# Key loads on another queue, and the heads' projection and some tables at another place, in a four-layer graph network

## The chip, the cores and the metric

The kernel runs on one core of one Trainium2 chip. The metric is the device time of one launch in microseconds (us). The engines are PE (matrix multiplication, with PEld for its weight loads), DVE (the vector engine), ACT (the scalar engine), POOL (GpSimd) and SP (SyncE, which here only issues DMAs). A DMA is issued by the instruction queue of SP, ACT or POOL, and each of these works through its instructions in order: a DMA whose semaphore is not there yet holds everything behind it on that queue.

## The reference

The input is 16 graphs of 1024 nodes with 64 channels, and a weighted adjacency matrix of 1024 x 1024 for each. Four layers follow each other; after each comes `x = layernorm(x + layer(x))`.

```
# layer 0: batch norm, then a residual graph convolution
d = A.sum(2);  A_norm = sqrt(d)[:, :, None] * A * rsqrt(d)[:, None, :]
out = leaky_relu((I - A_norm) @ (batchnorm(x) @ W + b))

# layer 1: attention with 8 heads of 64 channels, gated with the adjacency
attn = softmax(g0 * (q @ k.T) * scale + g1 * A)        # g = exp(x @ W_gamma.T + b)
out  = concat_heads(attn @ v) @ W_proj.T + b_proj

# layer 2: quantiles over the neighbours, then an MLP
nd  = neighbours, thinned where a node has more than 32
s   = sort(where(nd, x, inf)) for each node and channel
agg = sum over tau, w in (.25, .25), (.5, .5), (.75, .25):
          w * (s[floor(pos)] + frac * (s[ceil(pos)] - s[floor(pos)])),  pos = tau * (nv - 1)
out = relu((x + agg) @ W1 + b1) @ W2 + b2

# layer 3
out = A @ (x @ W) + b
```

## The kernel before

A loop `for p in range(B // 2 + 1)`, fully unrolled, works on pairs of graphs, with the stages of three pairs in flight. One iteration holds, in this order:

1. the pool of the sort's keys is opened and `sort_keys` (L1157) loads the key tile (64 channels of two graphs on 128 partitions, 1024 nodes, 512 KB) of pair p-1 from `x2T_d` in HBM, with SP's queue;
2. `layer0` of the two graphs of pair p. `place_tables` (L310 to L317) loads two constant tables, `place` on SP and `identb` on ACT, and DVE makes `negidb` and `noteye` from the second. `layer0` loads x (L407, SP), normalizes it to y on DVE (L410, L411), transposes it on PE (L289), sums the adjacency's rows on ACT (L425, from tiles loaded by ACT's queue, L424), and `neighbours` walks over eight tiles of the transposed adjacency (`at`, L330, SP, four buffers), which give both the thinned neighbour matrix nd (L333, L334, L369) and the convolution's matmuls (L392);
3. `ends(p-2)`: layers 2 (its MLP) and 3 of pair p-2 (loads at L1022, L1023, L1056);
4. `attention(p)` for both graphs, with the sort of pair p-1's 1024 keys of each channel (55 compare-and-swap steps, L1105) beside it on DVE;
5. `quantiles(p-1)`, which finds the wanted neighbours of each node in the sorted order.

**The attention** of a graph runs in steps over head pairs and blocks of 128 queries: scores (L509), exponentials (L516, L524), transposes on PE (L531), and the weighted values (L545), which are a generator `parts` of two halves drained between the next step's transposes. When a graph's eight heads are ready, `heads(gr, k)` for k = 0 to 3 projects them for a quarter of the nodes: 32 matmuls into two PSUM banks (L562), two DVE products with the softmax's reciprocals (`t_pr`, L566), a sum over eight heads (L569), two adds (L570, L571) and the statistics of the layer norm; after k = 3 the norm is applied (L274, L277). For the first graph of a pair, `heads` is called in steps of the second one's attention. For the second graph, the four calls stand at the end of the attention, behind the last weighted values. Then x2 and its transpose are stored by POOL's queue.

**The quantiles** run over 96 steps: 16 groups of four channels, times 3 quantiles, times 2 graphs. In a step, PE makes the products V of nd with the nodes in sorted order, coded in words E (L774 to L779, L838, L847, L848), DVE compares them with limits (`compare`, lt, L853) to find the word in which the wanted rank lies, PE and ACT turn this into a one-hot matrix oh (`one_hot`, L862), DVE picks the words (`pick`, m, L870, twice 128x3072), and PE sums them (`sum_words`, wps). After eight steps of a unit, `kth_bit` finds the bit within the word by a search on DVE (r, L757). Twelve steps after a group's pick comes its lookup: `distances` (from r and the table `pen`), `least_values` and `sum_values` read the values back from tables `bd` and `base` by matmuls (L838) and copies on ACT (L900). Behind the last lookup, DVE scales the result (vals, L919) and POOL stores it (agg_d, L920).

What a unit needs ahead of its steps: `counts` and `limits` (the ranks per node, L659 to L667) and `weights(t)` (L676 to L684, cf among them, which is used from L919 and by the search) for t = 0 to 2; and for each four groups `load_values`, which clears `bd` and `base` with memsets, multiplies `bv` by a constant into `base` on DVE, and has POOL issue eight small DMAs into `bd`. Before the loop over the steps stand the three `weights` and the first three `load_values`.

The order on the engines is set in two ways: a scheduler orders instructions by data and buffers (a tile's slot must be released first), and an order written out by hand, `then`, ties PE's instructions into a sequence. A dependency with `in_order` orders two instructions of one engine and adds no semaphore.

Of the kernel before, what the change touches and what calls it, by code (L numbers as in the profile page):

```python
# [15 lines left out]
BF = mybir.dt.bfloat16  # L16
# [5 lines left out]
ALU = mybir.AluOpType  # L22
AX = mybir.AxisListType
PSUM = bass.MemoryType.PSUM

P = 128
# [12 lines left out]
GB = 4  # L39
# [71 lines left out]
def gnn_kernel(ctx: ExitStack, tc: tile.TileContext, a: dict, out: bass.AP):  # L111
    nc = tc.nc
# [51 lines left out]
    tones4 = load("tones4", [P, 4], F16, a["c_tones4"])  # L164
# [38 lines left out]
    x2T_d = dram.tile([B // 2 * P, N], F32, name="x2T_d")  # L203
# [11 lines left out]
    in_order = mybir.DependencyInfo(mybir.DependencyClass.NoSync, mybir.DependencyReason.DATA)  # L215
# [93 lines left out]
    def place_tables(l0):  # L309
        place = l0.tile([P, 8 * P], BF, name="place")  # L310
        nc.sync.dma_start(place, a["c_place"])
        identb = l0.tile([P, P], BF, name="identb")
        nc.scalar.dma_start(identb, a["c_idb"])
        negidb = l0.tile([P, P], BF, name="negidb")
        nc.vector.tensor_scalar(negidb, identb, -1.0, None, op0=ALU.mult)
        noteye = l0.tile([P, P], BF, name="noteye")
        nc.vector.tensor_scalar(noteye, negidb, 1.0, None, op0=ALU.add)  # L317
        return place, identb, negidb, noteye
# [152 lines left out]
    def attention(nat, ip, graphs, wqkv, x2, beside):  # L471
# [4 lines left out]
        with (tc.tile_pool(name="att", bufs=2, reuse_waits="tile") as att,  # L476
# [75 lines left out]
            def heads(gr, k):  # L552

                if k == 0:
                    nc.vector.reciprocal(gr.sm, gr.sm)
                smv = gr.sm.rearrange("p (f k) (q h) -> p h k f q", f=2, h=2)
                t = att1.tile([P, 2, 2, 4, C], F32, name="t_pr")
                pr = [bank([P, 2, 4, C]) for h in range(2)]
                for f in range(2):
                    for hp in range(H // 2):  # L560
                        for h in range(2):
                            then(nc.tensor.matmul(pr[h][:, f, hp, :],  # L562
                                                  gr.o[hp][HALF[h], (4 * f + k) * P:(4 * f + k + 1) * P],
                                                  wp[HALF[h], hp, :], start=True, stop=True))
                for h in range(2):
                    nc.vector.tensor_tensor(t[:, :, h], pr[h],  # L566
                                            smv[:, h, k, :, :, None].to_broadcast([P, 2, 4, C]), ALU.mult)
                x = gr.xg[:, k]
                nc.vector.tensor_reduce(x, t.rearrange("p f h q c -> p f c (h q)"), AX.X, ALU.add)  # L569
                nc.vector.tensor_tensor(x, x, bp_r[:, None, :].to_broadcast([P, 2, C]), ALU.add)  # L570
                nc.vector.tensor_tensor(x, x, gr.x1[:, k], ALU.add)  # L571
                if k == 0:
                    gr.norm = norm_tiles()
                norm_stats(gr.norm, gr.xg, [k])
                if k == 3:
                    norm_apply(gr.norm, by_half(x2)[:, :, :, gr.bb, :], gr.xg)

            g0, g1 = graphs
# [15 lines left out]
            parts = iter(())  # L594
            for st, (gr, hp, nh, k4) in enumerate(steps):
# [26 lines left out]
                if gr is g0 and hp == H // 2 - 1:  # L622

                    k = 4 * nh + k4
# [4 lines left out]
                if (nh, k4) in ((0, 2), (1, 0)):  # L629
                    if hp + 1 < H // 2:  # L630
                        project(gr, hp + 1, nh)
                    elif gr is g0:
                        project(g1, 0, nh)
            for _ in parts:
                pass
            for k in range(4):
                heads(g1, k)
            nc.gpsimd.dma_start(x2_d[ds(ip * P, P)], x2)
            x2T = att1.tile([P, N], F32, name="t_pr")
# [142 lines left out]
    def quantiles(ip, rk, u_w, b_w):  # L782
# [12 lines left out]
        with ExitStack() as es:  # L795
# [10 lines left out]
            def load_matrix(gr):  # L806
# [4 lines left out]
                for c4 in range(4):  # L811
                    for pc in range(3):
                        nc.gpsimd.dma_start(gr.bv[c4::4, :, pc:pc + 1],
                                            scratchb[gr.r, pc, :].rearrange("(g k) (t u) -> k t g u", k=4, u=1)[c4])

            def load_values(gr, gb):


                bd = gr.bd[gb] = qn.tile([P, 2, GB, P], F16, name="bd", bufs=3)
                nc.vector.memset(bd, 0.0)  # L820
                gs = slice(GB * gb, GB * (gb + 1))
                for c4 in range(4):
                    p4 = slice(c4 * 32, (c4 + 1) * 32)
                    for pc in range(2):
                        nc.gpsimd.dma_start(
                            bd[c4::4, pc, :, p4],
                            scratch[gr.r, pc, :].rearrange("(g k) (t u) -> k t g u", k=4, u=R)[c4][:, gs])
                base = gr.base[gb] = qn.tile([P, GB, 3, 60], F16, name="base", bufs=3)
                nc.vector.memset(base, 0.0)
                nc.vector.tensor_tensor(base[:, :, :, 28:32], gr.bv[:, gs, :, None].to_broadcast([P, GB, 3, 4]),  # L830
                                        tones4[:, None, None, :].to_broadcast([P, GB, 3, 4]), ALU.mult)

# [32 lines left out]
            def pick(u, s):  # L865
                gr, g, q = u.pairs[s]
                u.m = [None, None]
                for kk in range(2):
                    u.m[kk] = qe.tile([P, NW, N], BF, name="m", bufs=2)
                    nc.vector.tensor_tensor(u.m[kk], gr.V[g].bitcast(BF),  # L870
                                            u.oh[s][:, kk, None, :].to_broadcast([P, NW, N]), ALU.mult)

            def sum_words(u, s):
# [38 lines left out]
            def sum_values(u, s):  # L912
# [4 lines left out]
                if s == U8N - 1:  # L917
                    res = qn.tile([P, 512], F32, name="vals", bufs=5)
                    nc.vector.tensor_tensor(res, u.acc, gr.cf[u.n % 3], ALU.mult)  # L919
                    nc.gpsimd.dma_start(agg_d[gr.bb][:, u.n, :], res)  # L920

            pairs = [(gr, g, q) for gr in graphs for g in range(G) for q in range(NQ)]
            groups = [(gr, g) for gr in graphs for g in range(G)]
            units = [SimpleNamespace(n=i // U8N % NU, pairs=pairs[i:i + U8N], oh=[], vals={}) for i in range(0, len(pairs), U8N)]
# [34 lines left out]
                counts(hf)  # L959
            for q in range(NQ):  # L960
                limits(q)
            for t in range(3):
                weights(t)
            more_words(4)
            compare(*steps[0])
            one_hot(*steps[0])
            pen = qn.tile([P, U8N, 3, P], F16, name="pen")
            nc.sync.dma_start(pen, a["c_pen"])
            lookups = [(gr, gb) for gr in graphs for gb in range(G // GB)]
            for _ in range(3):  # L970
                load_values(*lookups.pop(0))
            search = None
            for i, (u, s) in enumerate(steps):
                if i == 3 * NQ:
# [7 lines left out]
                gb, at = divmod(i - U8N - 2 * NQ, GB * NQ)  # L982
                if at == 0 and gb >= 1 and lookups:
                    load_values(*lookups.pop(0))
                look = steps[i - U8N - PARTS] if i >= U8N + PARTS else None
                more = MORE[s]
                pick(u, s)
# [166 lines left out]

    def sort_keys(srt, ip):
        key = srt.tile([P, N], F32, name="key", bufs=2)
        nc.sync.dma_start(key, x2T_d[ds(ip * P, P)])  # L1157
        return key

    def middle(keys, srt, key, pace=()):  # L1160
# [99 lines left out]
```

## Time and profile before

| | us |
|---|---|
| three runs | 13429.87, 13438.83, 13460.58 |
| median | 13438.83 |
| profiled execution | 13430.77 |
| its span in the profile | 13428.9 |

| engine | busy, us | share |
|---|---|---|
| PE | 12106.3 | 90% |
| DVE | 10731.4 | 80% |
| ACT | 7230.1 | 54% |
| POOL | 635.6 | 5% |

An iteration takes about 1645 us: the first quantile words E follow the attention at 1204.7, 2846 and 4491 us. PE's granted clock is 0.948 of full speed in the mean. A line such as "PE bank L838 <- DVE r L757: 18.2, 1, 18.2" in the waits says that PE at line 838 was idle for 18.2 us in total, once, until DVE finished r at line 757. In the timeline each line is start, length, engine, source line, operation, what it writes and reads, and in brackets the idle time before it.

### The profile page before, as it was taken

The numbers are of one execution on the slowest core, as the hardware profiler recorded it, in microseconds if no ns is written. First come the engines' busy times: TensorE is split into PE (matmuls) and PEld (weight loads), VectorE is DVE, ScalarE is ACT, GpSimd is POOL, SyncE is SP. The second block draws the span as 40 slices with busy tenths as digits, with TensorE's granted clock in tenths as the row PEclk, the third lists the DMA queues.
The fourth block names the chain that finished last, engine by engine and source line by source line (L and its number), as shares of the span: only waits on it lengthen the run. The fifth ranks groups of instructions, "written<-read, shape, count | busy, mean of one in ns | idle before, by whom it ended". The sixth has DMA issues, their size and how long they took to land.

```text
span 13428.9 us, 216352 instructions
## 1 busy us (share of the span) xinstructions
PE 12106.3 (90%) x85632; PEld 5237.5 (39%) x85632; DVE 10731.4 (80%) x18699; ACT 7230.1 (54%) x13164; POOL 635.6 (5%) x948
## 2 busy tenths in 40 slices
PE   7898997989979899798997989979899799993998
PEld 4554332543325433253333633335333353331332
DVE  3587887778877788777886788877888778978895
ACT  5665554655536555365553655546455465551553
POOL 0000000000000000000000010000100001000000
PEclk9999998999989999899998999989999899996998
DMA  2110003100031000310004100041000310002001
GB/s 78 69 63 19 5 5 105 57 17 5 5 121 42 15 6 5 131 34 14 5 5 132 32 14 5 5 134 38 6 5 20 121 36 7 8 22 77 4 5 44
DMA packets 356375, 510.90 MB, mean 38 GB/s; under 512 B 124448, under 2 KB 279584, under 8 KB 353312
## 3 DMA queue, kind: packets, MB, share of 16 engines
q1 hardware_dynamic: 288656, 371.94, 8.6%
q10 hardware_dynamic: 34192, 87.14, 1.9%
q0 software_dynamic: 32512, 38.00, 1.1%
q8 instruction: 673, 11.03, 0.3%
q14 instruction: 342, 2.80, 0.1%
HBM read 380.32 MB, written 116.59 MB: 37 GB/s over the span
## 4 chain that ended last, share of the span: by engine, by line
PE 66%; DVE 14%; issue 8%; DMA 3%; ACT 3%; POOL 0%; SPq 0%; DVEq 0%; ACTq 0%; POOLq 0%
PE bank L838 31%; PE acc L838 8%; PE banks L509 6%; PE bank L545 6%; PE bank L531 6%; PE wps L838 3%; DVE m L870 2%; DMA at<-in_adjT 2%; DVE key L1105 2%; PE bank L392 1%; PE bank L488 1%; PE banks L369 1%; PE bank L847 1%; DVE lt L853 1%; DVE mask L1105 1%
## 5 line engine op out<-in xcount | busy, mean ns | idle before, releaser
L870 DVE TENSOR_TENSOR m<-V,oh 128x3072 bf16<-128x3072 bf16 x1536 | 2640.2, 1753 | 312.9 <-PE wps L838 289.3
L838 PE MATMUL bank<-ndT,E 128*128 128x512 fp8e4 x11904 | 2751.7, 381 | 7.3
L900 ACT ACTIVATE vals<-bank 128x512 f32<-128x512 f32 x3072 | 1591.8, 602 | 1399.0 <-PE bank L838 1397.0
L516 DVE CUSTOM_DVE_ANT_0 s<-banks,adj 128x1024 f32<-128x1024 f32 x1024 | 1214.5, 1222 | 801.4 <-PE banks L509 798.4
L848 ACT ACTIVATE V<-bank 128x512 uint16<-128x512 f32 x1536 | 911.8, 597 | 1742.1 <-PE bank L838 1642.4
L838 PEld LDWEIGHTS <-E 128*128 128x128 bf16 x11904 | 1117.9, 98 | 1788.6 <-issue 551.0
L862 ACT CAST oh<-bank 128x512 f16<-128x512 f32 x3072 | 1577.6, 601 | 297.5 <-PE bank L838 297.3
L838 PE MATMUL bank<-oh,bd 128*128 128x512 f16 x6144 | 1480.0, 384 | 0.0
L535 ACT COPY pT<-bank 128x512 f32<-128x512 f32 x1536 | 800.6, 594 | 800.0 <-PE bank L531 799.9
L524 ACT ACTIVATE s<-s,mx 128x1024 f32<-128x1024 f32 x1024 | 1176.8, 1161 | 90.1 <-DVE mx L516 89.2
L509 PE MATMUL banks<-kT,qT 64*128 64x512 f32 x4096 | 1094.5, 625 | 65.7 <-DVE mx L516 36.1
L853 DVE TENSOR_TENSOR lt<-V,lim 128x2048 bf16<-128x2048 uint16 x768 | 935.1, 1218 | 221.5 <-PE bank L838 220.3
L531 PEld LDWEIGHTS bank<-ident,s 128*128 128x128 f32 x8192 | 883.9, 141 | 409.9 <-issue 285.7
L531 PE MATMUL bank<-ident,s 128*128 128x128 f32 x8192 | 1017.0, 277 | 9.3 <-ACT s L524 8.7
L545 PE MATMUL bank<-pT,v 128*64 128x256 f32 x8192 | 991.7, 385 | 0.0
L838 PEld LDWEIGHTS <-bd 128*128 128x128 f16 x6144 | 542.6, 98 | 889.4 <-issue 354.2
L838 PE MATMUL bank<-lt,dif 128*128 128x512 bf16 x3072 | 813.2, 381 | 51.9 <-DVE lt L853 30.9
L838 PE MATMUL acc<-vals,bonesf 128*32 128x512 f32 x6144 | 847.6, 603 | 0.0
L838 PE MATMUL wps<-m,tonesb 128*32 128x512 bf16 x9216 | 641.6, 382 | 78.7 <-DVE m L870 78.7
L838 PE MATMUL bank<-r,pen 32*128 32x512 f16 x6144 | 487.7, 384 | 241.0 <-DVE r L757 226.9
L545 PEld LDWEIGHTS bank<-pT,v 128*64 128x64 f32 x8192 | 544.7, 136 | 306.9 <-ACT pT L535 41.3
L838 PE MATMUL acc<-oh,base 128*32 128x512 f16 x9216 | 641.8, 384 | 0.0
(248 smaller groups left out, 13323.0 us busy)
## 6 DMA issues: line engine op xcount, KB each, us to landing
at<-in_adjT SPq DMA_DIRECT2D x256, 512.0 KB, 5.5
masks_d<-mask SPq DMA_DIRECT2D x440, 128.0 KB, 1.7
mask<-masks_d SPq DMA_DIRECT2D x440, 128.0 KB, 2.1
adj<-in_adj SPq DMA_DIRECT2D x96, 512.0 KB, 5.3
ad<-in_adj ACTq DMA_DIRECT2D x64, 512.0 KB, 6.4
agg_d<-vals POOLq DMA_DIRECT2D x96, 256.0 KB, 2.3
agg<-agg_d ACTq DMA_DIRECT2D x16, 1536.0 KB, 8.0
nd_d<-nd SPq DMA_DIRECT2D x128, 128.0 KB, 1.9
```

Of the source, the lines that this page charges most:

```text
L509: then(nc.tensor.matmul(ss[h][:, hf * 512:(hf + 1) * 512], gr.qk[hp, 0][HALF[h], k * P:(k + 1) * P], gr.qk[hp, 1][HALF[h], hf * 512:(hf + ...
L516: last = nc.vector.tensor_tensor_reduce(s, ss[h], gr.adj[k], -1.0, 3.0e38, ALU.add, ALU.min, mx)
L524: then_act(nc.scalar.activation(s, s, AF.Exp, bias=mx, scale=-1.0, accum_out=sm))
L531: then(nc.tensor.transpose(ps[:, m, :], exps[h][0][:, (4 * mh + m) * P:(4 * mh + m + 1) * P], ident))
L535: then_act(nc.scalar.copy(dst, ps))
L545: then(nc.tensor.matmul(po[HALF[h]], gr.v[:, 4 * mh + m, (2 * hp + h) * C:(2 * hp + h + 1) * C], pT[h][mh][:, m, :], start=(mh == 0 and m ...
L838: then(nc.tensor.matmul(*args, **kw))
L848: nc.scalar.activation(gr.V[g][:, w, cols], ps, AF.Copy, bias=OFF)
L853: nc.vector.tensor_tensor(u.lt, gr.V[g][:, None, 0, :].to_broadcast([P, 2, N]), gr.lim[q], ALU.is_lt)
L862: nc.scalar.copy(oh[:, kk, cols], ps)
L870: nc.vector.tensor_tensor(u.m[kk], gr.V[g].bitcast(BF), u.oh[s][:, kk, None, :].to_broadcast([P, NW, N]), ALU.mult)
L900: nc.scalar.activation(vals[t], ys[t], AF.Relu)
```

## The change

Five edits:

- `identb` is loaded by SP's queue and not by ACT's.
- In `heads`, the sum over eight heads (a reduction of 128x1024 to 128x128) is written as three adds of 128x512, 128x256 and 128x128.
- At the end of the attention, the first half of the last weighted values is followed by `heads(g1, 0)` and `heads(g1, 1)`, then comes the second half, then `heads(g1, 2)` and `heads(g1, 3)`.
- In `quantiles`, the first three `load_values` stand in steps 2, 4 and 6, and `weights(1)` and `weights(2)` in steps 10 and 12; the DVE instructions of `load_values` are ordered behind the latest pick.
- `sort_keys` loads the key by POOL's queue and not by SP's.

```diff
-        nc.scalar.dma_start(identb, a["c_idb"])
+        nc.sync.dma_start(identb, a["c_idb"])
...
                 x = gr.xg[:, k]
-                nc.vector.tensor_reduce(x, t.rearrange("p f h q c -> p f c (h q)"), AX.X, ALU.add)
+                nc.vector.tensor_tensor(t[:, :, 0], t[:, :, 0], t[:, :, 1], ALU.add)
+                nc.vector.tensor_tensor(t[:, :, 0, 0:2], t[:, :, 0, 0:2], t[:, :, 0, 2:4], ALU.add)
+                nc.vector.tensor_tensor(x, t[:, :, 0, 0], t[:, :, 0, 1], ALU.add)
...
+
+            next(parts)
+            for k in range(2):
+                heads(g1, k)
             for _ in parts:
                 pass
-            for k in range(4):
+            for k in range(2, 4):
                 heads(g1, k)
...
+            def behind(i):
+                tc.add_manual_dep(i.ins, picked.ins.name, in_order, reason="after a pair's words")
+
             def load_values(gr, gb):
                 bd = gr.bd[gb] = qn.tile([P, 2, GB, P], F16, name="bd", bufs=3)
-                nc.vector.memset(bd, 0.0)
+                behind(nc.vector.memset(bd, 0.0))
...
-                nc.vector.memset(base, 0.0)
-                nc.vector.tensor_tensor(base[:, :, :, 28:32], gr.bv[:, gs, :, None].to_broadcast([P, GB, 3, 4]),
-                                        tones4[:, None, None, :].to_broadcast([P, GB, 3, 4]), ALU.mult)
+                behind(nc.vector.memset(base, 0.0))
+                behind(nc.vector.tensor_tensor(base[:, :, :, 28:32], gr.bv[:, gs, :, None].to_broadcast([P, GB, 3, 4]),
+                                               tones4[:, None, None, :].to_broadcast([P, GB, 3, 4]), ALU.mult))
...
-            for t in range(3):
-                weights(t)
+            weights(0)
...
-            for _ in range(3):
-                load_values(*lookups.pop(0))
...
+                if i in (2, 4, 6):
+                    load_values(*lookups.pop(0))
+                if i in (10, 12):
+                    weights(i // 2 - 4)
...
         key = srt.tile([P, N], F32, name="key", bufs=2)
-        nc.sync.dma_start(key, x2T_d[ds(ip * P, P)])
+        nc.gpsimd.dma_start(key, x2T_d[ds(ip * P, P)])
```

More of the change, by code (lines that the diff above doesn't have):

```diff
@@ L867, in pick @@
                 u.m = [None, None]
+                nonlocal picked
                 for kk in range(2):
                     u.m[kk] = qe.tile([P, NW, N], BF, name="m", bufs=2)
-                    nc.vector.tensor_tensor(u.m[kk], gr.V[g].bitcast(BF),
+                    picked = nc.vector.tensor_tensor(u.m[kk], gr.V[g].bitcast(BF),
                                             u.oh[s][:, kk, None, :].to_broadcast([P, NW, N]), ALU.mult)
@@ L920, in sum_values @@
                     nc.gpsimd.dma_start(agg_d[gr.bb][:, u.n, :], res)
+            picked = None
             pairs = [(gr, g, q) for gr in graphs for g in range(G) for q in range(NQ)]
```

## The prediction

> **What bounds the kernel now.** I read the page's busy times and its chain first, then the chain, the waits and the timeline at the three places that the diff touches. 0.2% of the time is 27 us, about what a measurement of this kernel can tell from no change.
>
> ```profile
> PE 12106.3 (90%) x85632; PEld 5237.5 (39%) x85632; DVE 10731.4 (80%) x18699; ACT 7230.1 (54%) x13164; POOL 635.6 (5%) x948
> PE 66%; DVE 14%; issue 8%; DMA 3%; ACT 3%; POOL 0%; SPq 0%; DVEq 0%; ACTq 0%; POOLq 0%
> ```
>
> PE carries two thirds of the chain, and the change takes no matmul away. So it can win only where PE waits: at seams between stages, once per pair of graphs. None of these is large against a pair's 1645 us.
>
> Seam 1, the end of attention, from the chain of waits at 1160 to 1240 us (start, length, work):
>
> ```profile
> 1178.88 5.33 PE bank L545 x48
> 1184.22 1.98 PE bank L562 x32
> 1186.20 1.28 DVE t_pr L566 x2
> 1187.50 1.93 DVE xg L569
> ...
> 1191.50 1.79 DVE xg L569
> ...
> 1195.37 1.76 DVE xg L569
> ...
> 1199.20 1.75 DVE xg L569
> ...
> 1204.70 0.60 DVE E L774
> ```
>
> From 1186.2 to 1204.7 the vector engine works alone through four `heads` (L562 to L571) and the norm, and PE waits for it (the stretch holds 18.0 us of DVE in 18.7). The four reductions are 7.23 us of it.
>
> Seam 2, the start of the quantiles, 1231 to 1340 us, PE's waits (total, times, longest), then DVE's for 1224.4 to 1336.3:
>
> ```profile
> PE bank L838 <- DVE r L757: 18.2, 1, 18.2
> PE wps L838 <- DVE m L870: 4.7, 5, 2.3
> PE bank L838 <- DVE lt L853: 3.6, 4, 2.1
> ```
>
> ```profile
> DVE E L777 <- PE bank L838: 2.5, 2, 1.5
> DVE m L870 <- PE wps L838: 2.3, 2, 1.1
> DVE lt L853 <- PE bank L838: 1.5, 1, 1.5
> DVE E L779 <- PE bank L838: 0.5, 2, 0.3
> ```
>
> PE's long wait ends with the first search (r, L757, at 1336.4). Before it DVE idles 6.8 us in 112: DVE's own work sets when that search ends, not PE's.
>
> Seam 3, from the quantiles to the next pair's layer 0, the timeline at 2185 to 2232 us:
>
> ```profile
> 2196.45 0.33 SPq L1157 DMA_DIRECT2D key<-x2T_d  x1
> ...
> 2197.31 0.97 SPq L407 DMA_DIRECT2D x<-in_x  x2
> ...
> 2198.33 3.42 SPq L330 DMA_DIRECT2D at<-in_adjT  x4
> ...
> 2199.41 0.54 POOL L920 DMA_DIRECT2D agg_d<-vals  x1 [38.52 <-DVE vals L919]
> ...
> 2207.52 0.69 DVE L410 TENSOR_TENSOR y<-x,bn_a 128x512 f32<-128x512 f32 x1 [4.31 <-DMA x<-in_x]
> ```
>
> The key's load holds SP's queue for 32.1 us (SP's waits name PE, L838: the last lookup still reads `bd` in the key's space). The table, x and the first adjT tiles stand behind it, though their own buffers are free. They all start at 2196 to 2202, the DMA engines are then 96% busy at 326 GB/s until 2236 (windows), the last adjT tile of the graph is used at 2230.2, and PE waits 11.1 us for y.
>
> [...] the trace's 128x512 add takes 0.69. [...] in this trace x2T_d's stores on POOL land in 3.7 us and the key's loads on SP in 3.6[...]
>
> **The change part by part.** All sums are against the profiled execution: 13430.8 us (span 13428.9); the median of the other runs, 13438.8, is 8 us above it.
>
> *Adds for the reduction.* 128x512 costs 0.69 (key row, L1105), 128x256 0.42 (L428), 128x128 0.29 (L570): 1.40 against 1.81 in the tail, so 4 x 0.41 = 1.6 us per tail. The other 32 of 64 reductions lie beside PE-bound attention steps: nothing. *Order of heads.* Of the 48 L545 matmuls in 5.33 us, 16 now come after the first two heads, so the vector chain starts 5.33/3 = 1.8 us earlier. But PE then runs k=1's matmuls (which wait for a bank that t_pr frees), the 16, a copy on ACT (0.6) and k=2's 1.98 us, ready 7.1 us after the start, where DVE has done its two heads in 6.4: a new stall of 0.7. Tail: 1.6 + 1.8 - 0.7 = 2.7, with a step-by-step run of the chain 2.9; 1.5 if the order stalls more, 3.6 if not at all. Seven tails (pairs 1 to 7; pair 0's is counted below): **20 us** (10 to 25).
>
> *Later tables and weights.* Two of three `weights` (1.85 us each on DVE) and three `load_values` (1.04 each: two memsets and a product) move. Before, the load_values ran while DVE waited for PE and ACT at 1206 to 1228, for nothing; now 3.1 us of them stand inside DVE's full stretch, at steps 2, 4 and 6. The weights were in the stretch and stay in it (steps 10, 12). For that, the first compare no longer stands behind them: the picks and PE's steps begin some 4 us earlier (PE's 7.4 us a step, waits on lt and m less). What counts is the search: DVE's work after 1224.4 grows by 3.1, its 6.8 us of idle shrinks to perhaps 2.5. Gain 6.8 - 2.5 - 3.1 = 1.2 us; all idle gone +3.5, little of it gone -1.5. The lookups' DMAs (8 x 0.54 us of POOL per load) are wanted at step 12, 40 us after the last issue, and POOL has nothing else until then. Eight starts: **10 us** (-12 to 28).
>
> *Keys on POOL, the small table on SP, pairs 2 to 7.* SP is free from 2164: place, identb, x and four adjT tiles (2.5 MB) leave about 32 us earlier, in a third-busy DMA stretch (0.33 of 2150 to 2196). The key leaves on POOL behind the last agg_d store, about 2200.0 instead of 2196.45, and lands at 2203.7 to 2207. In the changed program's order DVE still has mask, key, y, key, y (L1105, L410, L411), so PE's first matmul follows the mask by 3.1 us: 2206.8 to 2210.1 against 2209.5, a gain of 0 to 2.7 where 4.3 of x's wait went. Behind that, 2.5 MB at 330 GB/s are 7.5 us less in the full stretch, but the `ad` tiles on ACT's queue, issued behind hnT, set the second y (2221.9), and four steps of 1.98 us follow: the adjT tail comes 2 to 4 us earlier, not 7.5. DVE is 96% busy at 2236 to 2306, so the shift carries on. I take 3 (-1 to 6); six times: **18 us** (-6 to 36). The identb edit alone is nothing: it leaves with the table, long before DVE reads it.
>
> *Pair 1.* There the key waits for its own data (x2T_d, 71.9 us of SP's wait) until 623.4, and DVE waits 12.6 for it; the key cannot come earlier, but adjacency and table can. They compete with x2T_d: **3 us** (0 to 7) beyond its tail. *The last pair.* No layer 0 follows; the key leaves behind the store, 3 us later, part of it covered by a 4.3 us wait on the masks: **-1** (-3 to 0).
>
> Sum 20 + 10 + 18 + 3 - 1 = 50: 13430.8 - 50 = **13381 us**. All ends good: 96, 13335; all bad: -10, 13441.
>
> **Rivals.**
> (A) *Everything lands.* Quantile starts keep the 4 us of PE's cadence because the search hides behind steps that PE still owes, and the DMA relief brings 6 each: 25 + 28 + 36 + 7 = 96 us, 13335. For it: PE is 90% busy; against: the 18.2 us wait on r.
> (B) *The seams swallow it.* DVE's idle refills behind PE (new waits on m), and the late key eats the earlier x: only tails count, 13411, or less where heads stall: within 0.2%. For it: three waits end together at 2207 to 2210.
> (C) *Slower: the late key.* POOL's path enters the full DMA stretch behind a 256 KB store (8.7 us until used, by the chain) and a 1.5 MB agg load; DVE's in-order mask holds y, and so all of layer 0. It decides where the mask starts after 2206.4 (2209.5 - 3.1). At a landing of 2213, 6.6 us late x 7 = 46, with 3.1 x 8 = 25 of load_values uncovered against 20 of tails: 13431 + 46 + 25 - 20 = 13482; with the threshold just passed, 13440 to 13460. Against it: SP's key landed in 3.6 to 4.0 among the same loads.
> (D) *The change does not do what it says:* tiles' slots still hold x and adjT until 2196. The program's waits for these name work long done, so I give it little; it would cost seam 3's 18: 13399.
>
> **How the numbers follow.** Forecast and D, gains of 28 to 75: 0.57; A: 0.13; B: 0.18; C: 0.12. Faster by over 0.2% takes the forecast and A: 0.70; same: 0.18; slower: 0.12. The range runs from A's end, 13335, to 13435, B and the near part of C.
>
> **What would show it.** In the profile after: DVE adds of 0.69, 0.42 and 0.29 us at the tail and E (L774 before) about 2.9 us sooner after the last transposes; L838's wait on r a little shorter (15 to 18 us) and the first wps 4 us earlier; SP's x and adjT issued near 2165, key on POOL near 2200, y not waiting for x, DMA share under 0.9 at 2196 to 2236. I am wrong if the key's mask starts over 10 us after the last vals, if DVE's time from lim to r grows, or if k=2's matmuls wait over 2 us.

## The result, and the profile after

| | before | changed |
|---|---|---|
| median of 12 runs, us | 13448.07 | 13444.57 |
| lowest and highest, us | 13429.87, 13460.58 | 13422.64, 13458.61 |
| ratio changed : before, 95% interval | | 0.9997 (0.9990 to 1.0005) |
| profiled execution, us | 13430.77 | 13445.01 |

The change makes no difference that can be measured: 4 us faster, with an interval from 13 faster to 7 slower. I had forecast 13381, 50 us faster, in a range of 13335 to 13435; the gain did not come and the time lies outside the range. The profiled execution of the kernel before is one of its fastest, 17 us below the median of 12, so the two profiles are compared place by place and never by their spans. Ratios below are turned into us with 13446.

The page after, busy time of each engine (before: PE 12106.3, DVE 10731.4):

```profile
PE 12131.7 (90%) x85551; PEld 5255.1 (39%) x85632; DVE 10695.0 (80%) x18827; ACT 7227.6 (54%) x13164; POOL 637.3 (5%) x956
```

DVE has 36 us less to do, the same tasks otherwise, and the kernel is no faster. The three seams tell why. Line numbers of the kernel after are higher: L774 is L780, L838 is L847, L870 is L880, L1105 is L1117 and L1157 is L1169 there.

**Seam 1, the end of attention.** PE's timeline of the kernel after at 1186 to 1200 us, and four pairs of graphs later, at 7770 to 7790 us (start, length, line, operation, count):

```profile
1192.76 2.00 PE L562 MATMUL bank<-wp,o 64*128 64x64 f32 x30 [0.56 <-DVE t_pr L566]
1194.68 1.95 PE L545 MATMUL bank<-pT,v 128*64 128x256 f32 x16
...
7775.93 3.10 PE L562 MATMUL bank<-wp,o 64*128 64x64 f32 x30 [0.56 <-DVE t_pr L566]
7778.96 3.68 PE L545 MATMUL bank<-pT,v 128*64 128x256 f32 x16
```

The 16 matmuls of weighted values that were put between the heads take 1.95 us in the first place and 3.68 in the second, and the heads' 30 ahead of them 2.00 and 3.10. First the windows of both places (length, then busy time and count of PE, PEld, DVE, ACT and POOL, PE's granted clock, DMA share and GB/s), then what DVE waits for PE at 1190 to 1208 and at 7772 to 7796 us:

```profile
1192.76:1196.63 3.87, 3.87 (x48) 2.98 (x48) 3.73 (x10) 0.00 (x0) 0.00 (x0) 1.00 0.00 0
7776.60:7782.60 6.00, 6.00 (x40) 3.99 (x38) 5.06 (x15) 0.00 (x0) 0.00 (x0) 0.50 0.01 3
```

```profile
DVE t_pr L566 <- PE bank L562: 4.8, 1, 4.8
```

```profile
DVE t_pr L566 <- PE bank L562: 8.0, 3, 4.8
```

In the second place the clock is halved, and DVE waits 3.2 us more for PE. From the end of the last exponential to the first E, all seven tails of the kernel before last 26.97 us. After, four last 23.68 and three 26.91: 3.3 us won or nothing.

**Seam 2, the start of the quantiles**, from the first limit (lim) to the end of the first search (r). First the window of the kernel before, then that of the kernel after:

```profile
1224.40:1336.20 111.80, 82.10 (x449) 32.13 (x447) 104.09 (x141) 52.15 (x93) 11.25 (x19) 0.92 0.02 2
```

```profile
1229.80:1342.60 112.80, 82.36 (x449) 32.17 (x447) 106.97 (x150) 52.14 (x93) 12.94 (x24) 0.91 0.02 2
```

DVE's work grew by 2.9 us (nine instructions: the three load_values), its idle time fell from 7.7 to 5.8 only, and the stretch is longer, 112.6 in the mean of seven against 111.8.

**Seam 3, from the quantiles to layer 0.** Timeline of the kernel after at 2203 to 2219 us:

```profile
2204.85 0.34 ACTq L1038 DMA_DIRECT2D agg<-agg_d  x1
2204.91 0.69 DVE L929 TENSOR_TENSOR vals<-acc,cf 128x512 f32<-128x512 f32 x1 [38.43 <-PE acc L847]
...
2206.49 0.55 POOL L1169 DMA_DIRECT2D key<-x2T_d  x1
...
2214.53 0.69 DVE L1117 TENSOR_TENSOR mask<-key 128x512 f16<-128x512 f32 x1 [8.59 <-DMA key<-x2T_d]
2215.74 0.68 DVE L410 TENSOR_TENSOR y<-x,bn_a 128x512 f32<-128x512 f32 x1
...
2217.68 1.11 PE L289 MATMUL bank<-ident,y 128*128 128x128 f32 x4 [12.80 <-DVE y L411]
```

x is there long before, and nobody waits for it any more. But y stands behind the sort's first mask on DVE, and the mask waits for the key, which lands 8.0 us after its issue (3.6 before). The windows from the key's issue to its landing, before and after:

```profile
2196.50:2200.10 3.60, 1.89 (x20) 0.52 (x12) 0.69 (x1) 3.54 (x7) 0.54 (x1) 1.00 0.72 237
```

```profile
2206.50:2214.50 8.00, 0.00 (x0) 0.00 (x0) 0.00 (x0) 0.67 (x2) 0.54 (x1) 0.68 1.01 332
```

After, the DMA engines are full all that time and move 2.7 MB, of which the key is 0.5. PE's wait for y is 12.8 us, longer than the 11.1 it had. L289 starts 12.3 us behind the last vals in the mean of pairs 2 to 7, against 10.0.

**Pair 1**, timeline after at 612 to 643 us:

```profile
614.58 3.02 SPq L424 DMA_DIRECT2D adj<-in_adj  x6
619.77 0.54 POOL L651 DMA_DIRECT2D x2T_d<-t_pr  x1 [0.70 <-ACT t_pr L650]
...
632.56 0.54 POOL L1169 DMA_DIRECT2D key<-x2T_d  x1 [12.25 <-DMA x2T_d<-t_pr]
636.70 0.69 DVE L1117 TENSOR_TENSOR mask<-key 128x512 f16<-128x512 f32 x1 [18.65 <-DMA key<-x2T_d]
```

SP no longer waits, so 3 MB of adjacency leave ahead of the 512 KB store of x2T_d that the key itself needs. The store lands after 12.5 us (7.4 before), and DVE waits 18.7 us for the key (12.6 before).

### The profile page after: what moved, and what is told of

The parts are those of the page before. It is cut to its first block, busy times and chain, and to the rows that moved or that the text cites. A ratio compares the mean times of both kernels' runs of the same rounds, so it can differ in the third digit from the quotient of the medians.

```text
span 13443.2 us, 216369 instructions
## 1 busy us (share of the span) xinstructions
PE 12131.7 (90%) x85551; PEld 5255.1 (39%) x85632; DVE 10695.0 (80%) x18827; ACT 7227.6 (54%) x13164; POOL 637.3 (5%) x956
## 5 line engine op out<-in xcount | busy, mean ns | idle before, releaser
L880 DVE TENSOR_TENSOR m<-V,oh 128x3072 bf16<-128x3072 bf16 x1536 | 2639.4, 1752 | 290.9 <-PE wps L847 266.1
L847 PE MATMUL bank<-ndT,E 128*128 128x512 fp8e4 x11904 | 2751.4, 381 | 7.6
L847 PEld LDWEIGHTS <-E 128*128 128x128 bf16 x11904 | 1118.1, 98 | 1798.2 <-issue 561.1
L847 PE MATMUL bank<-oh,bd 128*128 128x512 f16 x6144 | 1482.7, 385 | 0.0
L509 PE MATMUL banks<-kT,qT 64*128 64x512 f32 x4096 | 1088.8, 623 | 68.2 <-DVE mx L516 38.0
L531 PEld LDWEIGHTS bank<-ident,s 128*128 128x128 f32 x8192 | 886.0, 141 | 400.7 <-issue 290.1
L531 PE MATMUL bank<-ident,s 128*128 128x128 f32 x8192 | 1017.6, 278 | 0.5 <-DVE pT L537 0.5
L847 PEld LDWEIGHTS <-bd 128*128 128x128 f16 x6144 | 543.1, 99 | 893.3 <-issue 360.4
L847 PE MATMUL bank<-lt,dif 128*128 128x512 bf16 x3072 | 819.9, 384 | 60.9 <-DVE lt L862 48.2
L847 PE MATMUL acc<-vals,bonesf 128*32 128x512 f32 x6144 | 849.4, 603 | 0.0
L847 PE MATMUL bank<-r,pen 32*128 32x512 f16 x6144 | 489.5, 386 | 243.3 <-DVE r L763 229.3
L847 PE MATMUL wps<-m,tonesb 128*32 128x512 bf16 x9216 | 644.4, 384 | 66.8 <-DVE m L880 66.7
L847 PE MATMUL acc<-oh,base 128*32 128x512 f16 x9216 | 642.1, 384 | 0.0
```

What stands on the lines that cost most here:

```text
L509: then(nc.tensor.matmul(ss[h][:, hf * 512:(hf + 1) * 512], gr.qk[hp, 0][HALF[h], k * P:(k + 1) * P], gr.qk[hp, 1][HALF[h], hf * 512:(hf + ...
L531: then(nc.tensor.transpose(ps[:, m, :], exps[h][0][:, (4 * mh + m) * P:(4 * mh + m + 1) * P], ident))
L847: then(nc.tensor.matmul(*args, **kw))
L880: picked = nc.vector.tensor_tensor(u.m[kk], gr.V[g].bitcast(BF), u.oh[s][:, kk, None, :].to_broadcast([P, NW, N]), ALU.mult)
```

## The experiments

All are timed against the kernel before on the same chip (its medians there are 13443 to 13447 us); the notation is ratio, interval, us. Four of the runs (e10, e11, e12, e18) have 5 executions each, the others 9 to 21. The ratios are not those of the medians: by medians the last row is -54 and e14_adds -30.

| run | edits against the kernel before | ratio (95%) | us |
|---|---|---|---|
| e1_heads | adds, order of heads | 0.9977 (0.9970 to 0.9983) | -31 |
| e14_adds | adds | 0.9975 (0.9967 to 0.9983) | -34 |
| e16_order | order of heads | 0.9997 (0.9989 to 1.0006) | -4 |
| e2_tables | weights and load_values late | 1.0009 (1.0003 to 1.0016) | +12 |
| e6_weights | weights late | 0.9981 (0.9974 to 0.9987) | -26 |
| e17_load_values | load_values late | 1.0027 (1.0017 to 1.0037) | +36 |
| e3_queues | key on POOL, identb on SP | 1.0018 (1.0011 to 1.0025) | +24 |
| e8_identb | identb on SP | 1.0019 (1.0012 to 1.0026) | +26 |
| e11_keys_pool | key on POOL | 1.0033 (1.0021 to 1.0046) | +44 |
| e5_key_act | key on ACT, pairs 2 to 8 | 1.0007 (0.9998 to 1.0015) | +9 |
| e4_keys_on_sp | the changed kernel, key on SP | 1.0007 (0.9999 to 1.0015) | +9 |
| e13_identb_both | identb on SP, a spare one on ACT | 1.0013 (1.0007 to 1.0020) | +17 |
| e15_identb_pinned | identb on SP, ad held behind hnT | 0.9993 (0.9984 to 1.0001) | -9 |
| e10_best | adds, order, weights, key on ACT | 0.9963 (0.9951 to 0.9976) | -50 |
| e12_heads_weights | adds, order, weights | 0.9952 (0.9939 to 0.9964) | -65 |
| e18_adds_weights | adds, weights | 0.9954 (0.9941 to 0.9966) | -62 |

The changed kernel is heads + tables + queues: -31 + 12 + 24 = +5, measured -4 (-13 to +7). So the question "where did 50 us go" has a plain answer: one group gained, two lost. What follows is why.

### The three groups apart

**e1_heads**: the diff's two edits in `heads` and at the attention's end, nothing else.

> The kernel before with the heads' edits alone (three adds, and heads in two parts). Theory 1 (the seams add up, and the changed kernel loses what the heads gain at the other seams): from the last transposes to E is 3.3 us shorter in each of seven tails, as in the changed kernel's trace, and pair 0's tail brings some 3 more: 23 to 27 us faster, ratio 0.998. Theory 2 (an earlier end of the attention is absorbed by later waits or by the clock of TensorE, whatever the other edits do): the same 3.3 us at each tail, but within 8 us of the kernel before in time.

31 us faster; theory 1 on the time. Its tails, though, were not all 3.3 us shorter: 23.7, 25.3 or 26.9.

**e2_tables**: the diff's edits in `quantiles` alone.

> The kernel before with the quantiles' edit alone (tables and weights of later lookups made in the first steps). Theory 1: from lim to the first r it is longer by 0.3 to 1.1 us, since DVE's work there grows by 3 us and its idle time shrinks by 2 only: 3 to 10 us slower over eight starts. Theory 2 (the prediction's): the idle time shrinks by 4 us, 10 us faster. Theory 3: it is free here, and the longer stretch in the changed kernel came from the other edits: no change within 3 us.

12 us slower, theory 1. lim to r lasts 112.5 us (111.8) in the mean of seven starts: DVE works 107.0 us of it and is idle 5.5 (104.1 and 7.7 before). At the eighth start it is 112.8 against 110.2, so the eight together are 7 us longer, inside the interval of 4 to 22.

**e3_queues**: the two changed DMA lines alone.

> The kernel before with the two queue edits alone (keys on POOL, identb on SP). Theory 1: for pair 1 the freed loads crowd out the store of x2T_d and the key's mask is 10 us later; for pairs 2 to 7 the key lands 8 us after its issue instead of 4, L289 is 2 us later each; for the last pair 5 us: 20 to 27 us slower, ratio 1.0015 to 1.002. Theory 2 (the prediction's): x's earlier load and the lighter DMA stretch win, 20 us faster. Theory 3: it is slower at these places, but the layer-0 stretch behind them gives it back: within 8 us.

24 us slower, theory 1. L289 is 12.1 us behind the last vals (10.0), the key lands in 7.8 to 8.3 us for pairs 2 to 8, and the delay does not vanish behind it: the attention starts 221.9 us after the last vals instead of 217.9 (means of six; single ones of the kernel before lie between 214.8 and 220.2).

**e4_keys_on_sp**: the changed kernel with one line back.

```diff
-        nc.gpsimd.dma_start(key, x2T_d[ds(ip * P, P)])
+        nc.sync.dma_start(key, x2T_d[ds(ip * P, P)])
```

> The changed kernel with the keys' load back on SP's queue and the rest as changed. Theory 1 (the key's queue eats the heads' gain): 20 to 25 us faster than the changed kernel, 15 to 22 faster than the kernel before; layer 0's first L289 stands against the last vals as in the kernel before (10.4 us), and 17 us after the norm for pair 1. Theory 2 (the losses come from elsewhere, the tables' edit or chance): like the changed kernel, within 8 us of the kernel before.

9 us slower than the kernel before, with an interval from 1 faster to 20 slower: theory 1 is out, and theory 2 did not name the cause. The key lost nothing here (its mask starts 1.1 us after vals), but L289 was still 11.8 us behind them. Of the queue edits only identb was left to cost time; with e8_identb below the sum is -31 + 12 + 26 = +7.

### Heads: the adds, not the order

**e14_adds**: heads in one part.

```diff
-                nc.vector.tensor_reduce(x, t.rearrange("p f h q c -> p f c (h q)"), AX.X, ALU.add)
+                nc.vector.tensor_tensor(t[:, :, 0], t[:, :, 0], t[:, :, 1], ALU.add)
+                nc.vector.tensor_tensor(t[:, :, 0, 0:2], t[:, :, 0, 0:2], t[:, :, 0, 2:4], ALU.add)
+                nc.vector.tensor_tensor(x, t[:, :, 0, 0], t[:, :, 0, 1], ALU.add)
```

> The three adds alone, with the heads in one part behind the last weighted values. Theory 1 (the sum of the prediction): 1.6 us of the 3.3 at each of eight tails, 13 us faster, the rest of the heads' 31 comes with the order. Theory 2 (the order of heads is what counts, since the chain on DVE starts earlier, and PE hides the rest): under 5 us faster. Theory 3 (the adds free DVE also inside the attention's steps): over 20 us faster.

34 us faster, all that both edits bring: theory 3, and the term of theory 1 with it. All seven tails are 25.31 us, 1.66 shorter, as the prediction's 4 x 0.41 said; that is 13 us over eight. The rest is inside the attention, where I had put nothing. PE's waits at 790 to 1178 us (total, times, longest), first of the kernel before:

```profile
PE banks L509 <- DVE mx L516: 5.0, 6, 1.1
PE bank L531 <- ACT s L524: 1.1, 1, 1.1
PE bank L488 <- DVE t_pr L566: 1.0, 1, 1.0
PE bank L488 <- DVE pT L537: 0.5, 1, 0.5
```

and of e14_adds:

```profile
PE banks L509 <- DVE mx L516: 7.0, 7, 2.9
PE bank L488 <- DVE pT L537: 0.5, 1, 0.5
PE bank L488 <- DVE t_pr L566: 0.3, 1, 0.3
```

The wait of the transposes (L531) for an exponential is gone, and that of L488 for the bank that t_pr frees fell to a third. (L509's 2.9 us wait is in the kernel before too, at 789 us, just outside the window; over pairs 2 to 7, L509's wait for mx is 3.4 us before and 3.7 with the adds.) From the first scores to the last exponential, PE's idle time in the attentions of pairs 2 to 7 is 5.8 us each before and 4.3 with the adds; it is 5.7 to 5.8 in all ten other kernels without the adds and 4.3 to 4.4 in all six others with them. So the reductions of the first graph's heads were not all beside the work: some held DVE in front of something that PE wanted next. 1.66 + 1.5 us over eight pairs are 25 us, inside the interval of 23 to 44.

**e16_order**: the reduction kept.

```diff
+            next(parts)
+            for k in range(2):
+                heads(g1, k)
             for _ in parts:
                 pass
-            for k in range(4):
+            for k in range(2, 4):
                 heads(g1, k)
```

> The heads in two parts alone, with the reduction. Theory 1 (the prediction's): the vector chain starts 1.8 us earlier and stalls 0.7: 1.1 us at each of eight tails, 9 us faster. Theory 2 ([...]3.68 us instead of 1.95 for 16 matmuls; the vector chain waits for them): tails fall on two lengths, one 1.6 us below and one up to 1.6 above the 26.97 of the kernel before: within 6 us of the kernel before.

4 us faster, within its interval of no change: theory 2 on the time, though its shorter length is not there. Six of seven tails are 27.6 us, longer than before, and the seventh is 26.1. With the adds as well (e1_heads, the changed kernel) the tails are 23.68, 25.32 or 26.91. The clock records tell the three apart: at 23.68 the clock is full up to the last of the 16 matmuls; at 25.32 it halves 0.1 to 0.2 us after their start, for 3.41 us; at 26.91 it halves 2.0 to 3.0 us ahead of them, while the second head call's matmuls run, for 6.83 us. At all of these early falls PE was idle for only 0.56 of the 3.41 us before (3.41 us is the shortest stretch of half clock seen), in its wait for t_pr, and worked nearly all the rest on the heads' matmuls (L562).

In the clock records, the stretches of half clock around the tails of these runs last 3.41, 6.83, 10.24, 13.65 or 17.07 us, one to five times 3.41, and the same instructions take 1.95 us in one place and 3.68 in another. Which length a tail gets differs from pair to pair and from run to run: in e10_best all seven are short. What makes the clock fall was not shown.

### Tables: the weights gain, the load_values lose more

**e6_weights**:

```diff
-            for t in range(3):
-                weights(t)
+            weights(0)
...
+                if i in (10, 12):
+                    weights(i // 2 - 4)
```

> The kernel before with weights(1) and weights(2) in steps 10 and 12, and the load_values left where they were. Theory 1 (the moved load_values, which had lain in DVE's idle time, are what made the tables' edit slow): lim to r is 2 us shorter than in the kernel before, about 110 us instead of 111.8, 10 to 20 us faster over eight starts. Theory 2 (DVE's idle time before the first search is set by PE's cadence, whatever stands in it; the weights only move within it): lim to r within 0.5 us of 111.8, no change within 6 us.

26 us faster: theory 1, and more than the 10 to 20 that it gave. The window of this run from lim to r:

```profile
1230.50:1339.00 108.50, 81.75 (x449) 32.20 (x447) 103.96 (x141) 52.11 (x93) 10.90 (x18) 0.92 0.02 2
```

DVE's work is what it was (104.0); its idle time fell from 7.7 to 4.5, and 3.2 us over eight starts are 26. The first pick hardly moves (7.9 us after the first limit, 8.8 before), but the second starts at 16.4 us instead of 19.4: the two late weights are worked off between the picks, and DVE's waits for PE at L777 and L870 fall from 4.8 to 2.0 us in this window.

**e17_load_values**: with the three weights before the loop, and the load_values behind the latest pick as in the change.

```diff
-            for _ in range(3):
-                load_values(*lookups.pop(0))
...
+                if i in (2, 4, 6):
+                    load_values(*lookups.pop(0))
```

> The first three load_values in steps 2, 4 and 6 behind the latest pick, and the weights left before the loop. Theory 1 (their 3.1 us stand in DVE's full stretch and displace nothing): lim to r 115 to 116 us instead of 111.8, 25 to 35 us slower over eight starts. Theory 2 (they fill idle time there when the weights are early, and only with late weights they cost): lim to r within 1 us of 111.8, within 8 us.

36 us slower, theory 1. Its window:

```profile
1235.30:1351.30 116.00, 82.56 (x449) 32.04 (x447) 107.09 (x150) 52.12 (x93) 12.98 (x24) 0.91 0.02 2
```

3.0 us more of DVE's work and 1.2 more of idle time: 4.2 at this start, 4.0 in the mean of seven, and 5.9 at the eighth: 34 us. The two edits add up: 36 - 26 = +10, together +12. Whether the place in the steps or the order behind the latest pick costs the 1 us of idle time was not tried apart.

### Queues: the small table and the key

**e8_identb**: the key still on SP.

```diff
-        nc.scalar.dma_start(identb, a["c_idb"])
+        nc.sync.dma_start(identb, a["c_idb"])
```

> The kernel before with identb on SP's queue alone, behind the blocked key. Theory 1 (one more DMA ahead of x on the blocked queue, and x lands later in the full DMA stretch): L289 is 1.6 us later behind the last vals at six transitions, as in the run with the keys on SP: about 10 us slower. Theory 2 (that 1.6 us came with the tables' edit): no change within 4 us.

26 us slower, for a load of 32 KB, more than either theory gave it: L289 is 12.4 us behind the last vals (10.0). Timeline at 2201 to 2217 us:

```profile
2202.21 0.42 SPq L313 DMA_DIRECT2D identb<-in_c_idb  x1
2202.68 0.97 SPq L407 DMA_DIRECT2D x<-in_x  x2
...
2203.33 0.69 DVE L919 TENSOR_TENSOR vals<-acc,cf 128x512 f32<-128x512 f32 x1 [38.38 <-PE acc L838]
...
2206.40 0.33 ACTq L424 DMA_DIRECT2D ad<-in_adj  x1
...
2214.04 0.69 DVE L410 TENSOR_TENSOR y<-x,bn_a 128x512 f32<-128x512 f32 x1 [5.76 <-DMA x<-in_x]
```

Without identb on ACT's queue the scheduler planned ACT anew: the second graph's first `ad` tile, 512 KB, leaves ahead of hnT, 2.4 us after the last vals (11.6 before; 2.3 in e4_keys_on_sp), into the full DMA stretch in which x is on its way. y waits 5.8 us for x (4.3), and the attention starts 6.2 us later.

**e13_identb_both**: identb on SP, and an unused copy of it on ACT's queue at the old place, meant to keep ACT's plan.

```diff
-        nc.scalar.dma_start(identb, a["c_idb"])
+        nc.sync.dma_start(identb, a["c_idb"])
+        spare = l0.tile([P, P], BF, name="spare")
+        nc.scalar.dma_start(spare, a["c_idb"])
```

> identb loaded by SP's queue and used from there, and a second, unused copy of it loaded by ACT's queue at the old place, so that the planned order of ACT stays as before (in the run with identb on SP alone the first ad load moved ahead of hnT on ACT and left 9 us earlier, at 2.4 us after the last vals instead of 11.6). Theory 1 (the 25 us of that run came from ad's 512 KB in front of x, not from identb's own load): x is used about as in the kernel before, L289 10 to 10.6 us after the last vals, within 8 us of the kernel before. Theory 2 (the place on SP ahead of x costs it): L289 12 us after the last vals, 15 to 25 us slower.

17 us slower, with L289 12.3 us behind the last vals, as theory 2 has it. But it does not tell the two theories apart, since the spare load did not hold ad back (it left at 1.9 us).

**e15_identb_pinned**: so ad was held by hand, for pairs 2 to 7.

```diff
+                if not adj and ip >= 2 and k == 0:
+                    tc.add_manual_dep(load.ins, ahead[0].ins.name, in_order, reason="behind hnT")
```

(`ahead[0]` is the first graph's copy to hnT.)

> identb on SP's queue alone, with the first ad load of the second graph ordered behind the first graph's hnT on ACT for pairs 2 to 7, where the kernel before has it. Theory 1 (ad's 512 KB ahead of x made the run with identb on SP slow): ad leaves 11 to 13 us after the last vals, x lands near 8.5 us, L289 10 to 10.6 us after the last vals, within 8 us of the kernel before. Theory 2 (the DMA ahead of x on SP's queue and the changed order of the rest): L289 12 us after them, 15 to 25 us slower.

Timeline at 2212 to 2227 us (L424 is L428 and L919 is L925 here):

```profile
2212.82 0.69 DVE L925 TENSOR_TENSOR vals<-acc,cf 128x512 f32<-128x512 f32 x1 [37.57 <-PE acc L844]
...
2225.18 1.11 PE L289 MATMUL bank<-ident,y 128*128 128x128 f32 x4 [12.40 <-DVE y L413]
...
2226.34 0.33 ACTq L428 DMA_DIRECT2D ad<-in_adj  x1
```

9 us faster, within its interval of no change: theory 1 on the time, though not on the place. L289 is 11.4 us behind vals in the mean of six, so of the 2.4 us that e8_identb lost there only 1.0 goes with ad; x still lands 1.3 us later than in the kernel before, behind identb. But the eighth nbt ends 31.1 us behind vals (33.5 in e8_identb, 30.8 before), and the attention starts at 218.2 us, as before (217.9). With ad back in its place the 26 us are gone; most of what its early load had cost lay behind L289, not in the wait for x.

**e11_keys_pool**: identb left on ACT.

```diff
-        nc.sync.dma_start(key, x2T_d[ds(ip * P, P)])
+        nc.gpsimd.dma_start(key, x2T_d[ds(ip * P, P)])
```

> The kernel before with the key on POOL's queue alone, identb left on ACT. Theory 1 (each queue edit costs by itself; the late key of the changed kernel holds y): the mask starts 9 us after the last vals and L289 12 us after them, 2 us later than in the kernel before, pair 1 some 6 us later, the last pair 5: 15 to 25 us slower, as with both queue edits. Theory 2 (with both, it is identb that costs, and the key on POOL is even): within 8 us of the kernel before, though the mask is late, as the lighter DMA stretch gives it back before the attention.

44 us slower, more than theory 1 gave it. The key lands in 9.5 to 10.4 us for pairs 2 to 7 and L289 is 13.8 us behind vals. In this plan two of the four adjT tiles leave SP only 0.8 us ahead of the last vals, and so in front of the key, where the run with both queue edits has all four gone 24 us before. In that run the first ad tile is not early either: it leaves 13.4 us behind vals. So with both edits neither of the two plans that cost most alone comes about, and together (+24) they cost no more than either alone (+26, +44). Why the plans differ is open.

**e5_key_act**: the key on ACT's queue for pairs 2 to 8.

```diff
-        nc.sync.dma_start(key, x2T_d[ds(ip * P, P)])
+        (nc.scalar if ip else nc.sync).dma_start(key, x2T_d[ds(ip * P, P)])
```

> The kernel before, with the key loaded by ACT's queue for pairs 2 to 8 and by SP's for pair 1. Theory 1 (the freed loads are worth what the prediction said, and the key's time of issue decides: POOL issued it 3.5 us later, behind the store of vals and the load of agg): the key leaves about 1 us later than on SP, its mask starts 2 to 3 us after the last vals, L289 follows it by 3 to 4 us, so 5 to 6 us after the last vals instead of 10: 4 to 5 us at six transitions, 25 to 35 us faster. Theory 2 (the early loads of x and adjT only move the crowd, and the key lands as late as on POOL): L289 stays 10 to 12 us behind the last vals, no change or slower by up to 15 us.

Theory 1 was right about the place and wrong about the time. Timeline at 2199 to 2208 us:

```profile
2199.71 0.34 ACTq L1157 DMA_DIRECT2D key<-x2T_d  x1
...
2203.18 0.69 DVE L1105 TENSOR_TENSOR mask<-key 128x512 f16<-128x512 f32 x1 [1.05 <-DMA key<-x2T_d]
2204.59 0.68 DVE L410 TENSOR_TENSOR y<-x,bn_a 128x512 f32<-128x512 f32 x1
...
2206.54 1.11 PE L289 MATMUL bank<-ident,y 128*128 128x128 f32 x4 [5.14 <-DVE y L411]
```

The key leaves 2.4 us ahead of the last vals, before the load of agg, and lands in 3.4 us; L289 starts 4.4 us behind vals, 5.6 sooner. So an early key on ACT's queue lands as fast as on SP's, and POOL's own key of pair 1 in the changed kernel, issued at 632.56 when the freed loads were through, took 4.1: the time of issue accounts for the late key, and POOL's queue as such need not. (A key issued early on POOL was not tried, so a share of POOL's own store of vals, which goes ahead of the key, is not excluded.) And yet the attention starts at 218.8 us (217.9), no earlier than before, and the time is 9 us longer, with an interval from 3 shorter to 20 longer. DVE's waits in the 65 us behind the last vals, of the kernel before at 2199 to 2264 us:

```profile
DVE nbt L333 <- DMA at<-in_adjT: 8.1, 4, 3.2
DVE y L410 <- DMA x<-in_x: 4.3, 1, 4.3
```

and of e5_key_act at 2202 to 2267 us:

```profile
DVE nbt L333 <- DMA at<-in_adjT: 10.2, 4, 5.7
...
DVE mask L1105 <- DMA key<-x2T_d: 1.1, 1, 1.1
```

The wait for x became a longer wait for adjT: the eighth nbt ends 29.0 us behind vals (30.8), so 1.8 of 5.6 us are left there, and behind that the plans differ too much to follow the rest. That the early start is given back in the layer-0 stretch is shown; which later wait takes the last 1.8 us is not.

### The versions that gain

**e10_best**, **e12_heads_weights** and **e18_adds_weights** join the edits that gained.

> The heads' edits of the change, the key on ACT's queue for pairs 2 to 8 (SP's for pair 1), identb on ACT's queue, the weights late and the load_values early. If the effects add up as theory 1 has them, 31 + 30 + 15 = 76 us faster than the kernel before, near 13370; if only the heads' edits are worth something, near 13413.

> The heads' edits and the late weights, with the load_values, the key and identb as in the kernel before. Theory 1 (seams add up): 31 + 26 = 57 us faster than the kernel before, near 13386, and at least as fast as the run that also had the key on ACT (51). Theory 2 (the two gains overlap, since the second seam starts where the first ends): 35 to 45 us faster.

> The three adds and the late weights alone. Theory 1 (the order of heads is worth nothing): 30 + 26 = 56 us faster than the kernel before, like the run with the order as well (61). Theory 2 (the order helps where the clock is full): 10 us or more behind that run.

The key on ACT gains nothing here either: -50 with it, -65 without, with intervals that overlap. The adds and the late weights give -62, as much as with the order of heads. Both beat the kernel before and the changed one; e18_adds_weights gets there with the fewest edits, with a median of 13390.38 us.

## Why the prediction was wrong

1. **The adds: right at the tail, one term missing.** 1.6 us per tail was forecast, 1.66 measured. "The other 32 of 64 reductions lie beside PE-bound attention steps: nothing" failed: 1.5 us of PE's idle time per attention went with them. I took an engine that is busy for one that never waits. The evidence was in the trace before: PE's waits at L488 for t_pr and at L531 for the exponential, 1.0 and 1.1 us per pair.
2. **The order of heads: a size from a full clock.** 1.1 us net per tail was forecast, nothing measured. The step that failed is the chain on PE from k=1's matmuls over the 16 to k=2's, which I priced at full clock. Where the clock halves, k=1's take 3.10 us instead of 2.00, the 16 take 3.68 instead of 1.95, and k=2's and k=3's together 4.18 instead of 3.79: the 3.2 us by which those tails are longer. A stall of 0.7 us was allowed; DVE's is nil at full clock and 3.2 at half (2.1 in e16_order, where the reductions cover more of it). That the forecast of 20 us for both edits of the heads is near the 31 measured is luck: one term was too large and another was missing.
3. **Later tables: the idle term.** DVE's growth of 3.1 us was right (2.9 to 3.0). "Its 6.8 us of idle shrinks to perhaps 2.5" failed: with both parts moved it went from 7.7 to 5.5 us (e2_tables, mean of seven). Late weights alone take 3.5 us of idle away, late load_values give 1.0 back on top of their 3.0 us of work. I gave one number to two edits of opposite sign, and the forecast of -10 us was +12. The reason given failed too: "the first compare no longer stands behind them" was no change, since in the kernel before it already starts 1.0 us after the first limit and the weights follow it, and the picks begin 0.9 us earlier, not 4.
4. **Keys on POOL: the landing.** I issued the key at 2200.0 and let it land at 2203.7 to 2207; counted from the last vals that is 4.6 to 7.9 us, and it was 9.2 in the mean of pairs 2 to 7. The landing was my estimate from x2T_d's stores on POOL, which land in 3.7 us in a light stretch (DMA share 0.26 at 1204.6 to 1224.4 us); the key enters a full one (share 1.01, above), and pair 1's own store had taken 7.4. Rival C named this mechanism with its threshold (a mask after 2206.4, which is 7.3 us behind vals) and it was crossed at every pair, 9.2 us behind vals; I gave it 0.12, with the argument that SP's key landed in 3.6 to 4.0 "among the same loads". It did not: it left 1.9 us ahead of agg's 1.5 MB, and POOL's key leaves 1.6 us behind it. The same 512 KB took 8.0 us against 3.6, and 9.5 to 10.4 with two adjT tiles more in front; how the DMA engines divide their time between the transfers was not shown.
5. **The relief of the DMA stretch: absent.** Of 2 to 4 us nothing came: the eighth nbt is 2.3 us later with L289's 2.3.
6. **Pair 1: the sign.** Freed loads "compete with x2T_d: 3 us" was named as a compromise and was a loss. The mask is 6 us later behind the store than it was: 16.9 us from the store's issue against 10.8.
7. **identb "alone is nothing".** In the changed kernel it may be, since SP is free; alone it is 26 us slower, and most of that through a load that it does not touch. The place of `ad` in the planned order was left out of the account.

In the prediction's sum all bad ends make -11 and not -10; nothing hangs on it.

## What to carry to other kernels

Price each edit of a bundle by itself, and against the idle time that the profile before shows: here two gains of 34 and 26 us and two losses of 36 and 24 stood in one change and came to nothing. A queue that is held is also a gate: in the kernel before, SP's key waited 32.1 us, and place, x and four adjT tiles left within 5.3 us behind it. What you let out earlier runs ahead of the transfer on which the next stage waits (in pair 1, 3 MB of adjacency, and the 512 KB store landed after 12.5 us instead of 7.4), so price what will then stand in front of that one. Moving the awaited transfer first is not enough by itself: with the key early on ACT the next stage began 5.6 us sooner, and the kernel was no faster. Where a scheduler orders the program, compare the place of every large DMA after an edit, not only of the one that was edited.

## What the runs showed of the hardware

- 16 matmuls of 128x256 f32 into 64 columns take 1.95 us at the full and 3.68 us at the half clock, in the same program at the same place, pair by pair (granted clock 1.00 and 0.50). At these places the clock fell to half when PE had been idle for only 0.56 of the 3.41 us before.
- The key's 512 KB land in 3.2 to 4.2 us when the load is issued 2.1 to 2.7 us ahead of the last vals, on SP's and on ACT's queue, and in 7.8 to 9.0 us (with two adjT tiles in front of it 9.5 to 10.4) on POOL 0.9 us behind them, with the 1.5 MB of agg issued at least 1.6 us before.
- Three chained adds of 512, 256 and 128 columns (0.69, 0.42 and 0.29 us) do the work of a reduction of 1024 columns that takes 1.84 to 1.95 us.
